# A two-layer attention kernel on one core: GpSimd's queue, x's transfers and the last batch's logits rearranged

## The chip, the core and the metric

The kernel runs on one core of one Trainium2 chip. The metric is device time in microseconds (us) of one execution; the time before is the median of three runs. One further execution was recorded by the hardware profiler, and all lines and durations below come from it.

## What is computed

The input x holds 8 batches of 32 x 32 positions (1024 tokens) with 512 channels, in float32. Two layers follow each other:

```python
x = x + layer0(gn(x))   # 16 heads of 32: softmax(q k / sqrt(32)) v, then w_proj + bias
x = x + layer1(gn(x))   # 4 heads of 128: softmax(q k / sqrt(128) + pos) v, then Wo
```

`gn` is a normalisation over groups of 16 channels and all positions: minus the mean, divided by the root of the variance. `pos` is a relative position logit: for a query at (x, y) and a key at (x', y') it is the sum of a term that depends on the query and x' and one that depends on the query and y'.

## The kernel before, in words

**Tiling and stages.** Activations lie transposed, channels on the 128 partitions, as blocks of 128 x 4 x 1024 (eight block buffers in SBUF). A projection of 512 x 512 is done by a scheme of seven products in place of eight (`seven`, L457), whose operands are sums of quarters of the activations (`forming`, L388, four VectorE sums, L414) and of quarters of the weights (made once, kept in DRAM, and streamed in for every use by `Stream`). Each product is 8 matmuls, 1.7 us of TensorE.

The first layer's attention (`attention_0`) takes 64 steps per batch: logits on TensorE (L762), exp on ScalarE (L777), the values' matmul (L788), and VectorE adds the exponentials (L800). The second layer's attention (`attention_1`) takes 64 blocks per batch (4 heads x 2 column halves x 8 key tiles): ScalarE copies the block's position logits into PSUM (L928), TensorE adds q k onto them (L969), ScalarE takes exp (L971), TensorE multiplies with the values (L982), VectorE adds the exponentials (L996, L998).

**Position logits** of a block are the sum of two broadcasts. `Seeds` first stores both terms of each head into DRAM, spread out (L884, two stores of 512 KB a head, names pc and pr). Then it loads per block one tile of 256 KB (row, pos<-pr, L915) and per eight blocks one of 256 KB (columns<-pc), and GpSimd adds them in place (L920). Row tiles lie in eight slots, which are the `pos` tile itself; therefore all four heads' stores must have read `pos` before its slots can be overwritten. `put(i)` copies row i to PSUM, loads row i + 8, and has the adds up to row i + 2 issued.

**What sets the order.** The loop over b runs 9 times. In turn b, attention_0 of batch b is the frame, and between its steps `side_by_side` deals out, by a planned total of work, the rest: projection and residual of batch b-1 (`after_0`), the output projection of batch b-2 (`after_1`), normalisation (`norm_1`), the second layer's projections (`second`), attention_1 of batch b-1, and the projections of batch b+1 (`before_0`). The 64 blocks of attention_1 count nothing, so they run as one stretch, 64 x 1.72 us. In that stretch `load` of batch b+1 is woven in: x by DMA (L288, 32 transfers of 64 KB a batch), transposed on VectorE (L1068), statistics (L301, L302), stored (L270), the normalisation (`group_norm`), and the four sums. In turn 7 there is no next batch, and half of attention_1 runs beside attention_0; turn 8 has only the second layer of batch 7, and `after_last` ends the kernel.

Each engine, and SyncE, which issues nearly all DMAs, works through its own queue in order. A scheduler at build time chooses that order from the order in the program, and `tc.issue_after(ins)` places an instruction behind another of the same engine. `stream.behind` is such an anchor for the weights' loads: before, every DMA of `Seeds` set it.

**Lines that the change touches.** `statistics` takes a fresh tile mv of two buffers per normalisation and clears it on GpSimd (L298); that memset must wait until VectorE has read the buffer's last contents (L327). `group_norm` takes the root on GpSimd (rstd, L342), and L346 applies it on VectorE. `normalise` ends with a multiply (L743) on GpSimd for the first layer and on VectorE for the second. `Onto.add` (L643, L645) adds a product's result to the residual on VectorE, and `put_out` transposes it (L1282) and stores it (L1287). In `after_last` the final projection starts with two products whose operands need no sums and goes on with five that do; `ends` holds the closing part of the last attention (sum over keys, L1015, reciprocal, L743).

Of the kernel before, what the change touches and what calls it, by code (L numbers as in the profile page):

```python
# [17 lines left out]
P = 128  # L18
# [9 lines left out]
def quick_path(  # L28
# [103 lines left out]


# [132 lines left out]
    def put_away(xT, name):  # L266
        kept = []
        for cc in range(CC):
            d = dram.tile([P, N], F32, tag="kept", name=f"d_{name}_{cc}", bufs=4 * CC)
            put[0] = nc.sync.dma_start(d, xT[cc])  # L270
            kept.append(d)
        return kept
# [21 lines left out]
    def statistics(st, xT, cc, name):  # L294

        if "mv" not in st:
            st["mv"] = small.tile([P, 32], F32, tag="mv", name=f"mv_{name}", bufs=2)
            nc.gpsimd.memset(st["mv"], 0.0)  # L298
        s = small.tile([P, NH, 6], F32, tag="st", name=f"st_{name}_{cc}", bufs=2)
        for h in range(NH):  # L300
            nc.vector.bn_stats(s[:, h, :], xT[cc][:, h * NB : (h + 1) * NB])  # L301
        nc.vector.bn_aggr(  # L302
            st["mv"][:, : 2 * CC].rearrange("p (s c) -> p c s", c=CC)[:, cc, :],
            s.rearrange("p h s -> p (h s)"),
        )

    def group_norm(st, xT, name, after=None, behind=None, out=None):
# [32 lines left out]
        )  # L340
        rstd = small.tile([P, CC], F32, tag="rstd", name=f"rstd_{name}")
        nc.gpsimd.tensor_tensor(rstd, var, neg_half, op=ALU.pow)  # L342
# [15 lines left out]
    in_place = [False]  # L358

# [202 lines left out]
    def in_two_parts(  # L562
# [7 lines left out]
        def products():  # L570
            if in_turn:

                base = stream.at + 1
                parts = [two_first(early, u, sinks[u], f"{name}_{u}") for u in range(2)]
                for i in range(4):
                    stream.at = base + i % 2
                    yield next(parts[i % 2])
                for part in parts:
                    try:
                        next(part)  # L580
                    except StopIteration as end:
                        p1s.append(end.value)
                return
            for u in range(2):
                stream.unit(m, False, u)
                p1s.append((yield from two_first(early, u, sinks[u], f"{name}_{u}")))
# [43 lines left out]
    class Onto:  # L630
# [9 lines left out]
        def add(self, n, h, t):  # L640
            part = self.dst[n][h]
            if self.bias is None:
                nc.vector.tensor_add(part, t, part)  # L643
            else:
                nc.vector.scalar_tensor_tensor(  # L645
                    part, t, self.bias[n], part, op0=ALU.add, op1=ALU.add
                )
# [220 lines left out]
    class Seeds:  # L868
# [4 lines left out]
        def __init__(self, pos, b):  # L873
            self.pos, self.b = pos, b
            self.kept = []
            self.rows, self.columns, self.summed = {}, {}, 0
            self.last = None
            for h in range(H1):

                by_columns = dram.tile([4, 32, N], F32, tag="pos", name=f"pc_{b}_{h}", bufs=4 * H1)  # L880
                by_rows = dram.tile([32, 4, N], F32, tag="pos", name=f"pr_{b}_{h}", bufs=4 * H1)
                for u, to in enumerate((by_columns.rearrange("i x n -> x i n"), by_rows)):
                    rows = pos[32 * u : 32 * u + 32, h, :]
                    nc.sync.dma_start(to, rows.unsqueeze(1).to_broadcast([32, 4, N]))  # L884
                self.kept.append(
                    (by_columns.rearrange("i x n -> (i x) n"), by_rows.rearrange("y i n -> (y i) n"))
                )
# [6 lines left out]

        def load(self, i):
# [3 lines left out]
            h, c = divmod(group, NH)  # L899
            by_columns, by_rows = [d[:, c * NB : (c + 1) * NB] for d in self.kept[h]]  # L900
# [6 lines left out]
            to = self.rows[i] = self.pos[:, at // NH, (at % NH) * NB : (at % NH + 1) * NB]  # L907
# [4 lines left out]
        def bring(self, to, rows):  # L912

            with tc.issue_after(self.last.ins) if self.last is not None else nullcontext():
                self.last = stream.behind = nc.sync.dma_start(to, rows)  # L915

        def add_up(self, upto):
            while self.summed < min(upto + 1, H1 * NH * NT):
                i = self.summed
                nc.gpsimd.tensor_tensor(  # L920
# [4 lines left out]
        def put(self, i, ps):  # L925
# [4 lines left out]
            self.add_up(i + 2)  # L930

    def attention_1(q, k, v, seeds, b, beside=0, ends=None):
# [71 lines left out]
        def finish(h, c, esum):  # L1004
# [10 lines left out]
            nc.tensor.matmul(su, fold_flat, few, start=True, stop=True)  # L1015
# [5 lines left out]
        for i, at in enumerate(steps):  # L1021
# [15 lines left out]
            if i > 5:  # L1037
                stream.release()
            yield 0
# [5 lines left out]
        else:  # L1045
            for _ in range(2):
# [5 lines left out]
    def load(b, st):  # L1052
# [4 lines left out]
        with tc.issue_after(put[0].ins) if b == 1 else nullcontext():  # L1057
# [16 lines left out]
        if b > 1:  # L1074
            st["xn"] = yield from forming(x, f"xn0_{b}", behind=lambda: added[0])
            return
# [5 lines left out]
        for _ in range(2):  # L1082
            yield next(sums)
# [132 lines left out]
    def second(b, st):  # L1216
# [35 lines left out]
        def spread():  # L1252
            seeds.append(Seeds(pos, b))
# [3 lines left out]
            keys_and_values, chain(turn_over(1), position_logits(q, turned, pos, b), spread()), 0, 1  # L1257
        )
        seeds[0].add_up(3)
# [103 lines left out]
    SECOND = 3 * PRODUCT - 8 - 1  # L1363
# [44 lines left out]
    for b in range(B + 1):  # L1408
# [8 lines left out]
        def forms_0_apart(b=b, st=here):  # L1417
            st["ao0"] = yield from forming(st["q0"], f"ao0_{b}")
# [4 lines left out]
        if last is not None:  # L1423
# [23 lines left out]
            total += SECOND  # L1447
            shared = here is not None and coming is None
# [19 lines left out]
            rest.append(woven(attention, incoming, 4, 5))  # L1468
# [22 lines left out]
    pf = bank("pf", [P, 1])[:D0]  # L1491
# [485 lines left out]
```

## Time and profile before

| | us |
|---|---|
| median of 3 runs | 3710.1 (3709.67 to 3711.36) |
| the profiled execution | 3716.11 |
| its span, first to last instruction | 3714.2 |
| mean granted TensorE clock | 0.995 of full speed |

| engine | busy us | what it does most |
|---|---|---|
| ScalarE (ACT) | 2030.6 | exp L777 961.9, exp L971 305.1, copy L928 296.8 |
| GpSimd (POOL) | 1291.6 | adds L920 732.8 (512 of 1460 ns) |
| DMA queue of SyncE (q1) | 40.4% of 16 engines | 398.33 MB |

The page of a profile gives busy time and share of the span for each engine, the span in 40 slices, the DMA queues, the chain of work that ended last, and groups of instructions with what ended the idle time before them. PE is TensorE's matmuls, PEld its weight loads, DVE is VectorE, SPq SyncE's queue. A line "A <- B: t, n, m" of the view of waits says that A sat idle t us in all, n times, at most m, until B was done. A timeline line gives start, duration, engine, source line, operation, out<-in, how many, and in brackets the idle time before it and what ended it. L375 is the matmul of every projection; its tile names (x_q, y_wo, z_v) tell the product group and the matrix.

### The profile page before, as it was taken

The page shows a single profiled execution, that of the slowest core. Times are in us where ns is not written, and L with a number is a line of the kernel's source. Part 1 is how long each engine was busy: PE and PEld are TensorE (multiplying, and loading weights), DVE is VectorE, ACT ScalarE, POOL GpSimd, SP SyncE. Part 2 cuts the span into 40 slices and gives each one's busy share as a digit, 9 for nine tenths or more (in the row PEclk, how much of TensorE's full clock was granted, in tenths as well). Part 3 has the DMA queues.
Part 4 walks back from the last instruction along what each step waited for, and adds up shares of the span by engine and source line. Part 5 has one row for each costly group of instructions (what it writes and reads, how often), then busy time and mean ns, then how long its engine had stood idle before and what let it go on. Part 6 is the DMA issues. An engine that isn't in the chain of part 4 may idle for free.

```text
span 3714.2 us, 81237 instructions
## 1 busy us (share of the span) xinstructions
PE 3654.9 (98%) x33998; PEld 1247.2 (34%) x33998; DVE 2565.8 (69%) x2905; ACT 2030.6 (55%) x2281; POOL 1291.6 (35%) x847
## 2 busy tenths in 40 slices
PE   9999999999999999999999999999999999999998
PEld 4232243222433234332343323423234232333343
DVE  6778667686676857769576685767858677666445
ACT  2555665446654466544665456654566445655343
POOL 1352155131551316413172132811337022255254
PEclk9999999999999999999999999999999999999999
DMA  6122174132842338334372343813457132334384
GB/s 191 62 87 90 41 179 138 60 109 63 192 131 93 84 78 204 95 95 97 99 195 70 101 91 97 217 51 100 92 126 199 39 115 60 104 111 135 103 218 105
DMA packets 575158, 419.40 MB, mean 113 GB/s; under 512 B 279840, under 2 KB 471616, under 8 KB 573760
## 3 DMA queue, kind: packets, MB, share of 16 engines
q1 hardware_dynamic: 563152, 398.33, 40.4%
q0 software_dynamic: 2608, 13.70, 1.0%
q8 instruction: 270, 4.42, 0.5%
q10 hardware_dynamic: 9024, 2.10, 0.3%
q14 instruction: 104, 0.85, 0.1%
HBM read 321.72 MB, written 92.27 MB: 111 GB/s over the span
## 4 chain that ended last, share of the span: by engine, by line
PE 89%; DVE 5%; ACT 2%; DMA 2%; issue 1%; POOL 1%; SPq 1%; ACTq 0%; DVEq 0%; POOLq 0%
PE ps L762 14%; PE acc L788 13%; PE ps L969 10%; PE acc L982 10%; PE y_q L375 4%; PE y_k L375 4%; PE y_v L375 4%; PE z_q L375 3%; PE x_k L375 3%; PE x_q L375 3%; PE x_v L375 3%; PE z_k L375 3%; PE z_v L375 3%; PE y_wp L375 2%; PE y_wo L375 2%; PE x_wp L375 2%
## 5 line engine op out<-in xcount | busy, mean ns | idle before, releaser
L800 DVE TENSOR_TENSOR e_room<-e_room 128x2048 f32<-128x2048 f32 x448 | 1083.1, 2418 | 445.6 <-ACT e_room L777 443.1
L777 ACT ACTIVATE e_room<-ps 128x2048 f32<-128x2048 f32 x512 | 961.9, 1879 | 747.6 <-PE ps L762 716.7
L920 POOL TENSOR_TENSOR pos<-pos,columns 128x512 f32<-128x512 f32 x512 | 732.8, 1460 | 197.4 <-DMA pos<-pr 196.6
L762 PE MATMUL ps<-q,k 32*64 32x512 f32 x8192 | 594.6, 613 | 2.3 <-ACT e_room L777 2.3
L788 PE MATMUL acc<-e_room,v 128*32 128x512 f32 x4096 | 546.8, 604 | 1.0 <-ACT e_room L777 1.0
L982 PE MATMUL acc<-e,v 128*128 128x512 f32 x1024 | 527.1, 598 | 15.0 <-ACT e L971 14.5
L969 PE MATMUL ps<-q,k 128*128 128x512 f32 x1024 | 533.5, 604 | 6.7 <-ACT ps L928 6.6
L971 ACT ACTIVATE e<-ps 128x512 f32<-128x512 f32 x512 | 305.1, 597 | 267.6 <-PE ps L969 248.9
L998 DVE TENSOR_TENSOR es<-es,e 128x512 f32<-128x512 f32 x384 | 274.7, 715 | 159.8 <-ACT e L971 154.8
L928 ACT COPY ps<-pos 128x512 f32<-128x512 f32 x512 | 296.8, 590 | 75.0 <-POOL pos L920 36.2
L743 POOL TENSOR_TENSOR q<-q,su 128x512 f32<-128x512 f32 x64 | 104.6, 1634 | 528.8 <-DVE su L739 525.5
L982 PEld LDWEIGHTS acc<-e,v 128*128 128x128 f32 x1024 | 193.1, 191 | 269.9 <-issue 207.2
L969 PEld LDWEIGHTS ps<-q,k 128*128 128x128 f32 x1024 | 187.8, 191 | 242.5 <-issue 207.6
L762 PEld LDWEIGHTS ps<-q,k 32*64 32x64 f32 x8192 | 123.3, 129 | 398.2 <-issue 220.9
L788 PEld LDWEIGHTS acc<-e_room,v 128*32 128x32 f32 x4096 | 81.4, 108 | 412.2 <-issue 363.0
L628 POOL TENSOR_TENSOR k<-b_k,p_k 128x512 f32<-128x512 f32 x32 | 48.9, 1527 | 481.6 <-ACT p_k L479 481.6
L628 POOL TENSOR_TENSOR q<-b_q,p_q 128x512 f32<-128x512 f32 x32 | 60.2, 1881 | 384.3 <-ACT p_q L479 360.4
L628 POOL TENSOR_TENSOR v<-b_v,p_v 128x512 f32<-128x512 f32 x32 | 56.8, 1775 | 349.3 <-ACT p_v L479 349.3
L860 ACT COPY pos<-pp 32x512 f32<-32x512 f32 x128 | 104.3, 815 | 29.5 <-PE pp L851 28.3
L996 DVE TENSOR_TENSOR es<-e,e 128x512 f32<-128x512 f32 x64 | 74.3, 1161 | 63.7 <-ACT e L971 63.7
L704 DVE STREAM_TRANSPOSE tu<-su 128x512 f32<-128x512 f32 x64 | 45.1, 705 | 90.1 <-ACT su L702 90.1
L375 PE MATMUL y_q<-f_xn,w_q 128*32 128x512 f32 x768 | 92.9, 602 | 2.4 <-DVE a_q L465 2.4
(225 smaller groups left out, 4457.8 us busy)
## 6 DMA issues: line engine op xcount, KB each, us to landing
pos<-pr SPq DMA_DIRECT2D x512, 256.0 KB, 4.5
w_qkv<-ws_qkv SPq DMA_DIRECT2D x168, 128.0 KB, 2.6
d<-x0T SPq DMA_DIRECT2D x32, 512.0 KB, 5.1
x1T<-d SPq DMA_DIRECT2D x32, 512.0 KB, 5.1
d<-x1T SPq DMA_DIRECT2D x32, 512.0 KB, 3.5
pc<-pos SPq DMA_DIRECT2D x32, 512.0 KB, 7.0
pr<-pos SPq DMA_DIRECT2D x32, 512.0 KB, 8.2
columns<-pc SPq DMA_DIRECT2D x64, 256.0 KB, 5.3
```

What stands on the lines that cost most here:

```text
L375: ins = nc.tensor.matmul(out[columns, :], weights[:, columns], moving, start=start, stop=stop, skip_group_check=open_sum,)
L628: nc.gpsimd.tensor_tensor(self.dst[1][1], s(b), s(p7), op=ALU.add)
L762: nc.tensor.matmul(ps[some, r, :], k[m][rows, j * P + 64 * i : j * P + 64 * i + 64], q[m][rows, h * NB : (h + 1) * NB], start=True, stop=True,
L777: exps[0] = nc.scalar.activation(e, ps, AF.Exp, scale=D0 ** -0.5)
L788: nc.tensor.matmul(acc[r * D0 : (r + 1) * D0, :], v[:, j, c0 : c0 + D0], e[:, r, :], start=(j == blocks[0]), stop=(j == blocks[-1]),)
L800: summed[0] = nc.vector.tensor_add(state["esum"], state["esum"], e)
L920: nc.gpsimd.tensor_tensor(self.rows[i], self.rows[i], self.columns[i // NT], op=ALU.add)
L928: nc.scalar.copy(ps, rows)
L969: scored[0] = nc.tensor.matmul(ps, k[h][:, keys], q[:, h, queries], start=False, stop=True, skip_group_check=True)
L971: nc.scalar.activation(e, ps, AF.Exp, scale=1.0 / math.sqrt(D1))
L982: nc.tensor.matmul(acc, v[:, j, h * D1 : (h + 1) * D1], e, start=(j == 0), stop=(j == NT - 1),)
L998: added[0] = nc.vector.tensor_add(state["esum"], state["esum"], e)
```

## The change

- The mv tiles become two constant tiles, cleared once at the start and used in turn; the 16 memsets at L298 go.
- For batches 2 to 7 `load` is replaced by `load_apart`: three portions of x (4 transfers each) are fetched first and one after each transposed portion, each behind `stream.behind`; each quarter is stored as soon as it is transposed; the root on GpSimd is issued behind the newest logits add; the fourth sum moves to the start of `before_0`. The weaving into attention_1 goes from every fifth block to two of every seven.
- `put(i)` has the logits' adds issued up to row i + 4, not i + 2, and six before the attention, not four.
- `Seeds` takes an own block as room for the rows of the last batch; there only head 0 is stored before the first eight rows are loaded, and head h + 1 at the third row of head h. `stream.behind` is now set once per attention block, to the newest `Seeds` DMA.
- In the end: the closing part of attention_1 goes one step further before it is handed on (three steps, not two), its sums' matmul and the first products keep their order, the residual adds of the second pair of products stand behind the newest sum, and the verdict's matmul gets a PSUM room of its own.
- The sums between the two layers of batch 7 stand behind the newest softmax add, and the planned work grows by one unit where there is no previous or no next batch.

```diff
@@ consts
+    mvs = [consts.tile([P, 32], F32, tag=f"mv{i}", name=f"mv{i}") for i in range(2)]
+    for t in mvs:
+        nc.gpsimd.memset(t, 0.0)
@@ statistics
-            st["mv"] = small.tile([P, 32], F32, tag="mv", name=f"mv_{name}", bufs=2)
-            nc.gpsimd.memset(st["mv"], 0.0)
+            st["mv"] = mvs[0]
+            mvs.reverse()
@@ group_norm(..., apart=False)
+        if apart:
+            yield 0
         rstd = small.tile([P, CC], F32, tag="rstd", name=f"rstd_{name}")
-        nc.gpsimd.tensor_tensor(rstd, var, neg_half, op=ALU.pow)
+        with tc.issue_after(spread[0].ins) if apart else nullcontext():
+            nc.gpsimd.tensor_tensor(rstd, var, neg_half, op=ALU.pow)
@@ in_two_parts, in_turn
                 for i in range(4):
                     stream.at = base + i % 2
+                    if i == 0:
+                        in_place[0] = True
+                    behind_sums[0] = i > 1
                     yield next(parts[i % 2])
+                behind_sums[0] = False
@@ Onto.add
-                nc.vector.tensor_add(part, t, part)
+                with tc.issue_after(last_form[0].ins) if behind_sums[0] else nullcontext():
+                    nc.vector.tensor_add(part, t, part)
@@ Seeds
+            self.room = pos if room is None else room
...
+            if room is not None:
+                self.put_by(0)
+                for i in range(self.ROWS):
+                    self.load(i)
+                return
...
+            if h == len(self.kept) - 1 and h + 1 < H1 and c == 0 and j == 2:
+                self.put_by(h + 1)
...
-                self.last = stream.behind = nc.sync.dma_start(to, rows)
+                self.last = nc.sync.dma_start(to, rows)
...
-            self.add_up(i + 2)
+            self.add_up(i + 4)
@@ attention_1
-            nc.tensor.matmul(su, fold_flat, few, start=True, stop=True)
+            ins = nc.tensor.matmul(su, fold_flat, few, start=True, stop=True)
+            if ends is not None and (h, c) == steps[-1][:2]:
+                tc.keep_in_program_order(ins)
+                in_place[0] = True
...
+            stream.behind = seeds.last
...
-            for _ in range(2):
+            for _ in range(3):
                 next(last)
@@
+    def load_apart(b, st, parts):
+        def bring(i):
+            with tc.issue_after(stream.behind.ins):
+                return load_blocks(b, *parts[i])
+        ahead = [bring(i) for i in range(3)]
+        yield 0
+        x = block(f"x0T_{b}")
+        xT = chunks(x)
+        st["kept"] = []
+        for i, (cc, h) in enumerate(parts):
+            nc.vector.transpose(xT[cc][:, h * NB : (h + 1) * NB], ahead.pop(0))
+            if h == NH - 1:
+                statistics(st, xT, cc, f"0_{b}")
+                st["kept"] += put_away(xT[cc : cc + 1], f"0_{b}_{cc}")
+            yield 0
+            if i + 3 < len(parts):
+                ahead.append(bring(i + 3))
+        late = lambda: added[0]
+        yield from group_norm(st, xT, f"0_{b}", apart=True)
+        fs = st["xn"] = []
+        sums = st["sums0"] = forming(x, f"xn0_{b}", behind=late, into=fs)
+        for _ in range(3):
+            yield next(sums)
@@ second
-            seeds.append(Seeds(pos, b))
+            seeds.append(Seeds(pos, b, block(f"slots_{b}") if b == B - 1 else None))
...
-        seeds[0].add_up(3)
+        seeds[0].add_up(5)
@@ the loop over b
-            st["ao0"] = yield from forming(st["q0"], f"ao0_{b}")
+            st["ao0"] = yield from forming(st["q0"], f"ao0_{b}", behind=lambda: added[0])
...
-            rest.append(woven(attention, incoming, 4, 5))
+            if here is not None and coming is not None:
+                rest.append(woven(attention, incoming, 3, 7, (0, 4)))
+            else:
+                rest.append(woven(attention, incoming, 4, 5))
```

## The prediction

> **What bounds the kernel now.** I read the page first (busy shares), then TensorE's waits, then the timeline around each of those waits, and last the granted clock there. The page's first part:
>
> ```profile
> PE 3654.9 (98%) x33998; PEld 1247.2 (34%) x33998; DVE 2565.8 (69%) x2905; ACT 2030.6 (55%) x2281; POOL 1291.6 (35%) x847
> ```
>
> TensorE is busy 3654.9 of 3714.2 us. No edit removes a matmul, so only its idle time and slow time can be won. The view of waits, for TensorE (what it waited for: total, times, longest):
>
> ```profile
> PE acc L982 <- ACT e L971: 14.5, 8, 3.1
> PE ps L969 <- ACT ps L928: 6.6, 14, 1.3
> ...
> PE z_v L375 <- DMA w_v<-ws_v: 3.0, 1, 3.0
> PE sums L1015 <- DVE fw L712: 2.7, 1, 2.7
> ...
> PE y_wo L375 <- DVE f_wo L414: 2.2, 1, 2.2
> ```
>
> The top row is the second layer's attention: acc waits for exp. Within 960 to 3080 us it is five waits of about 1.84 us, one per batch, and at 572 us one of 3.07. The GpSimd timeline just ahead of the one at 1480 us shows who is late:
>
> ```profile
> 1463.31 3.89 POOL L920 TENSOR_TENSOR pos<-pos,columns 128x512 f32<-128x512 f32 x3
> 1473.69 0.12 POOL L298 MEMSET mv<- 128x32 f32 x1 [6.50 <-DVE turned L327]
> 1473.77 3.73 POOL L920 TENSOR_TENSOR pos<-pos,columns 128x512 f32<-128x512 f32 x3
> 1479.07 1.02 POOL L342 TENSOR_TENSOR rstd<-var,neg_half 128x4 f32<-128x4 f32 x1 [1.57 <-DVE var L338]
> ```
>
> A 0.12 us memset holds GpSimd for 6.50 us, the root for 1.57 + 1.02, and the logits' adds (L920) stand behind both. ScalarE's copy of the summed logits (L928) then waits 2.71 us at 1481.36, and its exp stands behind that copy. The last view is TensorE by stretches (length, TensorE busy, ..., granted clock, DMA share, GB/s):
>
> ```profile
> 569.00:582.00 13.00, 9.89 (x16) 3.77 (x15) 9.19 (x14) 6.35 (x12) 11.42 (x9) 0.74 0.92 285
> ...
> 1479.00:1485.00 6.00, 4.15 (x11) 1.65 (x10) 3.95 (x5) 3.31 (x6) 5.93 (x5) 1.00 0.92 306
> ...
> 3360.00:3374.00 14.00, 9.87 (x18) 4.11 (x17) 13.09 (x16) 4.34 (x8) 13.16 (x8) 0.76 0.48 136
> 3541.00:3564.00 23.00, 16.08 (x126) 6.51 (x119) 4.49 (x6) 6.56 (x12) 15.37 (x13) 0.85 0.74 207
> ...
> 3680.00:3704.00 24.00, 20.09 (x174) 5.59 (x166) 15.30 (x22) 1.17 (x2) 6.00 (x4) 0.93 0.39 56
> ```
>
> A wait of 1.85 us leaves the clock at 1.00, longer ones (3.07 at 572, 2.66 at 3365, 3.00 at 3549, 2.24 at 3681) are followed by half speed. A mean of 0.74 over 13 us is 2 x 0.26 x 13 = 6.8 us at half clock, so 3.4 us lost beside the wait; 3360 to 3374 likewise 3.4, 3541 to 3564 3.4, 3680 to 3704 1.7.
>
> The Trainium skill, "TensorE: Matmul & The Clock Gate", section "HAM oscillation", has the rule that idle gaps over about 3.4 us throttle TensorE. By it none of these gaps would, and my sum below would be smaller by the clock terms I count, 3.4 + about 2.6 + 1.7. The rows differ from it, and I go by the rows.
>
> **The change, part by part** (times of the profiled execution: span 3714.2, run 3716.1).
>
> *Memset and root (six batches).* The memsets waited 8.61, 4.53, 6.50, 4.02, 5.56 and 4.79 us in the six phases that prepare a later batch; two tiles cleared once leave no wait. The root now stands behind the last add traced. Behind the root's result stand only the normalising instructions (L346), traced three to four blocks of 1.72 us later, so its delay is hidden; if it were not, VectorE's sums, exp and TensorE would queue behind L346. Won: 3.07 + 3.4 at 572 us, and 5 x 1.84. **15.7.** Next late would be the row transfers: GpSimd waits for them 196.6 us in 129 waits, but the 4.20 us one at 1456.67 cost TensorE nothing. Bounds 12 to 16.
>
> *Adds four blocks ahead.* Here GpSimd's queue holds hardly anything but these adds, so a greater lead changes little; adds 4 and 5 now precede the 3.32 us multiply (L743) at 1419.36. Against it: in the stage of batch 7's first layer, L743 then stands behind adds that wait up to 4.9 us for rows. **0**, bounds 2 won to 3 lost.
>
> *x in portions.* Before, 20 of the 32 x transfers of a batch were issued from 1425 to 1458 and 12 earlier, beside the projections; now all 32 stand behind row transfers, 12 at once in block 3, then 4 every three to four blocks, and three of the four stores of x0T move forward. From 1420 to 1475 SyncE issued 63 transfers at about 0.55 us, 35 of 55 us; 15 more make 43. It fits. The transfer engines are tighter: share 0.91 at 204 GB/s; 12 x 64 KB + 3 x 512 KB = 2.3 MB are 11 us at that rate, 7.7 us at the 306 GB/s of 1479 to 1485. So rows come up to 6 us later (50 + 11 against 55). The cover: adds done by 1467.19 were copied at 1471.29 to 1473.52, and copies run ahead of their matmuls. Without cover a batch pays a wait like 1.84 or 3.07 + 3.4. Bounds 0 to 6 x 6.5; I take **2 lost** in total, nearest the row in which a 4.20 us delay was hidden. VectorE gets lighter there by one sum (L414, 1.2 to 1.8 us each), which moves beside the next projection's first product.
>
> *The last batch's own slots.* SyncE's timeline before:
>
> ```profile
> 3526.70 2.85 SPq L884 DMA_DIRECT2D pr<-pos  x1
> 3529.65 2.49 SPq L915 DMA_DIRECT2D columns<-pc  x1
> 3532.23 3.62 SPq L915 DMA_DIRECT2D pos<-pr  x2
> ...
> 3544.34 1.06 SPq L226 DMA_DIRECT2D w_v<-ws_v  x2
> ```
>
> Six stores go before the first row, eight before the value weights, which are ordered behind the rows (stream.behind) and land too late for z_v. TensorE loses 3.2 (ps) + 3.0 (w_v) + 0.7 (acc) + 3.4 (clock) = 10.3. Now the first row needs the first head's two stores only (issued 3519.09 and 3520.28), and the order behind rows is gone for these weights. Bytes ahead of the eighth row fall from 8 x 512 + 9 x 256 KB = 6.4 to 4.4 MB, at 195 GB/s 10 us less: it lands near 3541, when the attention starts. I take **8**; bounds 10.3 won to 3 lost: heads 2 and 3 are stored in blocks 10 and 26, 1 MB each, 5 us at the 209 GB/s of 3565 to 3640. Four waits of ps for copies there (2.4 us) may go by the earlier adds: **1**, bounds 0 to 2.4.
>
> *Tail.* VectorE before the last projection's second part:
>
> ```profile
> 3678.88 1.00 DVE L743 TENSOR_TENSOR q<-q,su 128x512 f32<-128x512 f32 x1
> ...
> 3679.87 0.68 DVE L643 TENSOR_TENSOR x2T<-x_wo,x2T 128x512 f32<-128x512 f32 x1
> 3680.47 1.21 DVE L414 TENSOR_TENSOR f_wo<-q 128x1024 f32<-128x1024 f32 x1
> 3681.60 0.70 DVE L1282 STREAM_TRANSPOSE ot<-x2T 128x512 f32<-128x512 f32 x1
> 3682.23 1.18 DVE L414 TENSOR_TENSOR f_wo<-f_wo,q 128x1024 f32<-128x1024 f32 x1
> ```
>
> y_wo waits for the second sum, done 3683.41, while TensorE is free at 3681.22. The sums' matmul comes one product (1.7 us) earlier, and the add and transpose (0.68 + 0.70) go behind the sums: ready about 3680.5. That ends 2.24 + 1.7; I take **3.5**, bounds 0 to 3.9. The 1.67 us wait of z_wo for ScalarE, which is issuing stores, stays.
>
> *Batch 7's first layer.* At 3358.70 the first sum (L414) holds VectorE 2.38 us for GpSimd's L743; TensorE then loses 1.5 + 2.7 + 3.4. The sum now stands behind the newest softmax add, so less is queued behind it, but it can still wait. I take **2**, bounds 3 lost to 7.6 won. One unit more of planned work in two stages and the verdict's own PSUM room: 0, within 1 either way.
>
> Sum: 15.7 + 0 - 2 + 8 + 1 + 3.5 + 2 = 28.2; 3716.1 - 28.2 = 3687.9. The profiled run is 6.0 above the median of 3710.1, so on the medians 3681.9: **3682**.
>
> **Rivals.**
> 1. *Transfers become the bound, mildly*: rows late by some 2.3 us of TensorE time per batch, clock kept: 6 x 2.3 = 14 more, 3696. For it: DMA share 0.91 and the 11 us above. Against: the hidden 4.20 us.
> 2. *The other side, slower*: the same place (blocks 8 to 30 of six attention phases), waits long enough to halve the clock. Price 3.3 + 3.4 = 6.7 per batch, 40 in all; without my 2, 3682 - 2 + 40 = 3720. It decides from (28 + 2) / 6 = 5.0 us lost per batch. Against it: rows are eight blocks ahead, 13.8 us, against 4.6 us to land.
> 3. *It does not do what it says*: the five short waits stay, because exp still stands behind a copy that waits for a late row, and the own slots bring nothing: 3682 + 9.2 + 8 = 3699.
> 4. *Little change*: memsets gone (15.7), but the end turns worse: the spread stores cost 3, batch 7's sums 3, the x loads 4, the tail gains nothing: 3710.1 - 15.7 + 10 = 3704.
>
> **How the numbers follow.** Chances: forecast 0.63, rival 1 0.14, rival 3 0.09, rival 4 0.07, rival 2 0.07. The low end is all bounds won, 16 + 2 + 10.3 + 2.4 + 3.9 + 7.6 = 42: 3668. The high end takes in rival 4: 3705; rival 2 is left out. A measurement tells 0.2% (7.4 us) from no change: under 3702.7 is faster (forecast, 1, 3: 0.86), rival 4 is the same (0.07), rival 2 slower (0.07).
>
> **What would show it.** Right: no wait of GpSimd for turned (L327) and none of acc near block 36 of each batch; clock 1.00 at 569 to 582; w_v issued before 3537 and no z_v wait; y_wo without its 2.2 us. Wrong: acc or ps waits around blocks 10 to 30, GpSimd's waits for pos<-pr well over 196.6 us, a half clock in each batch; or the last batch's ps waiting later on.

## The result, and the profile after

| | median of the runs | profiled execution |
|---|---|---|
| before | 3709.9 us (3703.2 to 3713.9, 12 runs) | 3716.1, span 3714.2 |
| after | 3720.2 us (3715.9 to 3722.1, 12 runs) | 3721.6, span 3719.7 |

The ratio is 1.0026, 95% interval 1.0017 to 1.0035: the change makes the kernel slower, by a little over 0.2%, where I had forecast 3682. Both times lie outside each other's range, and the forecast's range ended at 3705. The traced execution of the kernel before is slower than each of its 12 timed ones (its mean granted clock is 0.995, that of the trace after 0.997), so the two traces differ by 5.5 us only, the medians by 10.3.

Starts of the same exp in the two traces, subtracted, tell where it goes. The changed kernel is 0.5 us late before batch 1's second attention, loses 5.3 to 7.2 us more from each attention to the next, and stands 32.6 us late where batch 7's turn begins (3006.3 us before, 3039.0 after). Then it wins: 17.8 late at the last block of batch 6's attention, 8.4 at the last block of batch 7's, 5.5 at the end. So a gain of 27 us is there. It is eaten by what was lost ahead of it.

The page after, first part. TensorE's busy time is what it was; its time without work is 66.0 us (3719.7 - 3653.7), 59.3 before:

```profile
PE 3653.7 (98%) x33998; PEld 1243.8 (33%) x33998; DVE 2558.4 (69%) x2905; ACT 2025.6 (54%) x2281; POOL 1282.1 (34%) x833
```

Each kernel has its own line numbers. In the changed one the root is L350 (L342 before), the normalising L354 (L346), the key sum L727 (L712), the logits' add L946 (L920), ScalarE's copy L954 (L928), exp L997 (L971) and the softmax add L1024 (L998). TensorE's waits after (what for: total, times, longest):

```profile
PE ps L995 <- ACT ps L954: 16.5, 38, 1.2
PE sums L1041 <- DVE fw L727: 15.3, 12, 1.5
PE acc L1008 <- ACT e L997: 8.1, 13, 1.1
...
PE y_q L385 <- DVE a_q L475: 0.6, 1, 0.6
...
PE y_wo L385 <- DVE f_wo L424: 0.5, 1, 0.5
```

The old long waits are gone or short (acc was 14.5 with a longest of 3.1, y_q 2.4, y_wo 2.2, z_v is missing). Many shorter waits are there instead: ps for ScalarE's copies 38 times (0.4 us on average), sums for the key sums 12 times (1.3 us on average).

GpSimd in the same batch as before, around the root (start, length, ..., idle before and its releaser):

```profile
1487.64 7.12 POOL L946 TENSOR_TENSOR pos<-pos,columns 128x512 f32<-128x512 f32 x5 [0.20 <-DMA pos<-pr]
1496.92 3.83 POOL L946 TENSOR_TENSOR pos<-pos,columns 128x512 f32<-128x512 f32 x3 [2.16 <-DMA pos<-pr]
1500.71 1.02 POOL L350 TENSOR_TENSOR rstd<-var,neg_half 128x4 f32<-128x4 f32 x1
```

No memset waits, and the root waits for nothing of its own. But its input, the variance, was ready at 1496.5, and three adds stood ahead of it, which had just waited 2.16 us for a row. VectorE meanwhile:

```profile
1496.36 0.16 DVE L343 SCALAR_TENSOR_TENSOR var<-back 128x4 f32<-128x4 f32 x1
1496.44 2.30 DVE L1024 TENSOR_TENSOR es<-es,e 128x512 f32<-128x512 f32 x3
1501.77 1.75 DVE L354 TENSOR_SCALAR x0T<-x0T,back,rstd 128x1024 f32<-128x1024 f32 x1 [3.03 <-POOL rstd L350]
1503.44 0.69 DVE L1024 TENSOR_TENSOR es<-es,e 128x512 f32<-128x512 f32 x1
...
1507.42 1.12 DVE L354 TENSOR_SCALAR x0T<-x0T,back,rstd 128x1024 f32<-128x1024 f32 x1
1508.46 0.67 DVE L727 TENSOR_REDUCE fw<-tu 128x16 f32<-128x512 f32 x1
```

The first normalising instruction (L354) holds VectorE for 3.03 us, and softmax adds (L1024) and the key sum (L727) stand in its queue behind it. TensorE then waits 0.73 (acc), 1.48 (sums) and 0.42 us (acc) between 1504 and 1511. Its longest wait there, and VectorE's view of waits for this pair, which had 0.3 us before:

```profile
1509.19 0.40 PE L1041 MATMUL sums<-fw,fold 128*128 128x16 f32 x2 [1.48 <-DVE fw L727]
...
DVE x0T L354 <- POOL rstd L350: 17.2, 7, 3.4
```

The granted clock, in stretches that answer to those of before, and one more (the clock is the third number from the end):

```profile
569.00:582.00 13.00, 12.81 (x32) 5.78 (x32) 10.06 (x25) 9.54 (x18) 10.35 (x9) 1.00 0.78 213
...
1964.00:1972.00 8.00, 6.92 (x14) 3.05 (x15) 6.26 (x12) 3.79 (x7) 8.00 (x6) 0.79 0.41 130
3410.00:3424.00 14.00, 14.00 (x36) 6.35 (x35) 11.79 (x17) 9.94 (x17) 9.77 (x8) 1.00 0.58 183
3563.00:3586.00 23.00, 22.63 (x86) 10.12 (x79) 12.41 (x17) 15.73 (x27) 21.05 (x17) 1.00 0.67 185
```

The drops at 572, in batch 7's turn and at the last attention's start are gone. A new one, 3.4 us long (8 x 0.21 x 2) and 1.7 us lost, follows the cluster of waits in batches 3, 4 and 5, at 1966, 2423 and 2880, and none in batches 0 to 2.

SyncE at the last attention's start:

```profile
3541.40 0.96 SPq L231 DMA_DIRECT2D w_v<-ws_v  x1
3543.75 1.16 SPq L941 DMA_DIRECT2D slots<-pr  x2
3544.97 0.58 SPq L941 DMA_DIRECT2D pc<-pos  x1
3545.59 0.56 SPq L941 DMA_DIRECT2D pr<-pos  x1
3546.20 7.16 SPq L941 DMA_DIRECT2D slots<-pr  x6
```

The value weights are no longer behind eight stores: the second head's stores (L941, pc and pr) come later than they do, and TensorE no longer waits for them. And VectorE in the tail (the last projection), where the sums now go ahead of the add and transpose:

```profile
3685.58 1.05 DVE L758 TENSOR_TENSOR q<-q,su 128x512 f32<-128x512 f32 x1
...
3686.67 1.23 DVE L424 TENSOR_TENSOR f_wo<-q 128x1024 f32<-128x1024 f32 x1
3687.93 2.18 DVE L424 TENSOR_TENSOR f_wo<-f_wo,q 128x1024 f32<-128x1024 f32 x1
3690.04 0.68 DVE L658 TENSOR_TENSOR x2T<-x_wo,x2T 128x512 f32<-128x512 f32 x1
```

The sums now follow the multiply (L758) closely, and y_wo waits 0.5 us instead of 2.2, although the second sum takes 2.18 us where it took 1.18.

### The profile page after: what moved, and what is told of

It reads as the page before. It is cut to its first block, busy times and chain, and to the rows that moved or that the text cites. A ratio compares the mean times of both kernels' runs of the same rounds, so it can differ in the third digit from the quotient of the medians.

```text
span 3719.7 us, 81204 instructions
## 1 busy us (share of the span) xinstructions
PE 3653.7 (98%) x33998; PEld 1243.8 (33%) x33998; DVE 2558.4 (69%) x2905; ACT 2025.6 (54%) x2281; POOL 1282.1 (34%) x833
## 4 chain that ended last, share of the span: by engine, by line
PE 90%; DVE 3%; ACT 2%; POOL 2%; issue 2%; DMA 1%; SPq 0%; ACTq 0%; DVEq 0%; POOLq 0%
PE ps L777 14%; PE acc L803 13%; PE ps L995 10%; PE acc L1008 9%; PE y_v L385 4%; PE y_q L385 4%; PE y_k L385 4%; PE x_v L385 3%; PE z_q L385 3%; PE x_k L385 3%; PE x_q L385 3%; PE z_k L385 3%; PE z_v L385 3%; PE y_wp L385 2%; PE y_wo L385 2%; PE sums L825 2%
## 5 line engine op out<-in xcount | busy, mean ns | idle before, releaser
L946 POOL TENSOR_TENSOR pos<-pos,columns 128x512 f32<-128x512 f32 x448 | 640.5, 1454 | 212.4 <-DMA pos<-pr 205.6
L995 PE MATMUL ps<-q,k 128*128 128x512 f32 x1024 | 534.6, 605 | 16.5 <-ACT ps L954 16.5
L997 ACT ACTIVATE e<-ps 128x512 f32<-128x512 f32 x512 | 305.4, 597 | 310.2 <-PE ps L995 268.8
L1024 DVE TENSOR_TENSOR es<-es,e 128x512 f32<-128x512 f32 x384 | 278.0, 724 | 188.2 <-ACT e L997 181.2
L758 POOL TENSOR_TENSOR q<-q,su 128x512 f32<-128x512 f32 x64 | 107.2, 1674 | 558.0 <-DVE su L754 533.3
L954 ACT COPY ps<-pos 128x512 f32<-128x512 f32 x448 | 256.0, 590 | 36.9 <-PE ps L967 9.2
L719 DVE STREAM_TRANSPOSE tu<-su 128x512 f32<-128x512 f32 x64 | 45.2, 706 | 87.4 <-ACT su L717 87.2
L385 PE MATMUL y_q<-f_xn,w_q 128*32 128x512 f32 x768 | 91.3, 593 | 0.8 <-DVE a_q L475 0.6
```

The lines of the kernel that those rows point to most:

```text
L385: ins = nc.tensor.matmul(out[columns, :], weights[:, columns], moving, start=start, stop=stop, skip_group_check=open_sum,)
L946: spread[0] = nc.gpsimd.tensor_tensor(self.rows[i], self.rows[i], self.columns[i // NT], op=ALU.add)
L954: nc.scalar.copy(ps, rows)
L995: scored[0] = nc.tensor.matmul(ps, k[h][:, keys], q[:, h, queries], start=False, stop=True, skip_group_check=True)
L997: nc.scalar.activation(e, ps, AF.Exp, scale=1.0 / math.sqrt(D1))
L1024: added[0] = nc.vector.tensor_add(state["esum"], state["esum"], e)
```

## The experiments

My theory after the traces: the new preparation of x (portions, their order behind rows, root and sums placed anew) costs the 33 us; slots, tail and batch 7's turn win theirs. The rival: the adds four ahead, or full transfers, make logits late. A difference of some 3 us between two kernels lies within the runs' spread, so for those the traces are read as well.

**1. Preparation as before.**

```diff
-        if b > 1:
-            yield from load_apart(b, st, parts)
-            return
...
+        if b > 1:
+            st["xn"] = yield from forming(x, f"xn0_{b}", behind=lambda: added[0])
+            return
...
-                rest.append(woven(attention, incoming, 3, 7, (0, 4)))
+                rest.append(woven(attention, incoming, 4, 5))
```

> The changed kernel with the whole preparation of a later batch's x put back as it was before: the x transfers unordered, two portions ahead, the four stores together, root and normalising instructions free, the fourth sum in the attention; constant mv tiles, adds four ahead, the last batch's own slots and the tail stay. My theory: the loss of 32.7 us that the trace of the change shows from batch 1 to batch 6 comes from this preparation alone, and the 27 us won in batch 7's turn and at the end from the other parts, so 3720 - 33 = 3687 us (3680 to 3695). Rival (the adds four ahead, or GpSimd's queue as a whole, cost the time): little comes back, 3705 to 3720.

3671.8 us, ratio to before 0.9895 (0.9879 to 0.9911): 48.4 under the changed kernel. The preparation is the cause, and costs more than the 33 us that I read from the comparison with before, since that comparison already held gains: where batch 7's turn begins, this run is 16.6 us ahead of the kernel before (memsets and planned work, runs 6 and 14). This version beats both kernels. GpSimd's waits for rows fall to 161.9 us (205.6 after, 196.6 before).

**2. Portions of x not ordered behind rows.**

```diff
-            with tc.issue_after(stream.behind.ins):
+            with nullcontext():
                 return load_blocks(b, *parts[i])
```

> The changed kernel, but the portions of x are not ordered behind the row transfers. My theory: this order makes the scheduler place ScalarE's copies of the logits late and in bunches, right ahead of the exp that needs them, and TensorE waits for ps about 1.9 to 2.4 us a batch; without it the waits of ps for copies go and 6 x 1.9 to 2.4 = 12 to 14 us come back: 3707 us (3702 to 3712). The waits of acc and sums around the root stay. Rival (the rows themselves land late because the transfers and SyncE are full): no gain, or worse, 3718 to 3730, since x now goes ahead of rows.

3702.3 us, 0.9983 (0.9974 to 0.9992): 17.9 come back. TensorE's waits of ps for copies fall from 16.5 us in 38, while GpSimd waits for rows as long as in the changed kernel (205.6 us):

```profile
PE ps L995 <- ACT ps L954: 4.2, 14, 1.2
...
POOL pos L946 <- DMA pos<-pr: 204.6, 129, 6.7
```

So it was not late rows that cost this time. ScalarE in the changed kernel (blocks 22 to 24), and at blocks 22 and 23 in this one:

```profile
1466.66 0.60 ACT L997 ACTIVATE e<-ps 128x512 f32<-128x512 f32 x1 [0.63 <-PE ps L995]
1468.38 0.60 ACT L997 ACTIVATE e<-ps 128x512 f32<-128x512 f32 x1 [1.12 <-PE ps L995]
1470.10 0.60 ACT L997 ACTIVATE e<-ps 128x512 f32<-128x512 f32 x1 [1.12 <-PE ps L995]
1470.95 0.59 ACT L1027 COPY q<-acc 128x512 f32<-128x512 f32 x1 [0.26 <-PE acc L1008]
1471.44 1.63 ACT L954 COPY ps<-pos 128x512 f32<-128x512 f32 x3
```

```profile
1461.10 0.59 ACT L954 COPY ps<-pos 128x512 f32<-128x512 f32 x1
1462.13 0.60 ACT L997 ACTIVATE e<-ps 128x512 f32<-128x512 f32 x1 [0.44 <-PE ps L995]
1462.81 0.59 ACT L954 COPY ps<-pos 128x512 f32<-128x512 f32 x1
1463.85 0.60 ACT L997 ACTIVATE e<-ps 128x512 f32<-128x512 f32 x1 [0.44 <-PE ps L995]
```

Without the order one copy goes between two exps. With it ScalarE idles 1.12 us, twice, between exps that have no copy between them, and then does three copies in a row behind the copy of acc (L1027), with nothing that they wait for; their adds had been done 2.9 to 4.3 us earlier. So it is their place in ScalarE's queue that is late. Counted over the traces, the order is the same in all six attentions: in the changed kernel only one copy is left ahead at exps 13, 20, 24, 27, 31 and 34, in this run at 31 and 34, in the kernel before in most at exp 24 alone. That is what an order fixed when the program is built looks like. By the same exps, 3.0 us return by block 36 of each attention; behind it 1.3 to 3.1 us are lost again in batches 0, 1 and 2, where VectorE now waits up to 4.8 us for the root (25.8 us in 7 waits).

**3. Normalising behind the softmax add of its block.**

```diff
-        yield from group_norm(st, xT, f"0_{b}", apart=True)
+        yield from group_norm(st, xT, f"0_{b}", behind=late, apart=True)
```

> The changed kernel, but the four normalising instructions are ordered behind the softmax add of their own block. My theory: in the change the first of them stands right behind the variance on VectorE and holds it about 3 us while GpSimd's root waits behind adds that wait for rows; the softmax adds and key sums queue behind it, TensorE waits 2.6 us a batch for them and runs at half clock for 3.4 us in three of six batches (1.7 us lost each). So 6 x 2.6 + 3 x 1.7 = 21 us come back: 3699 us (3695 to 3708). Rival (VectorE's hold is hidden and the waits come from late copies): 3715 to 3722.

3700.7 us, 0.9978 (0.9969 to 0.9988): 19.4 come back, 2.0 to 4.9 us in the second half of each attention. The root's place is as it was; five softmax adds stand ahead of L354 now, and its wait at the same place is 1.06 us:

```profile
1492.28 3.90 DVE L1024 TENSOR_TENSOR es<-es,e 128x512 f32<-128x512 f32 x5
1497.24 1.75 DVE L354 TENSOR_SCALAR x0T<-x0T,back,rstd 128x1024 f32<-128x1024 f32 x1 [1.06 <-POOL rstd L350]
```

**4. All four sums in the attention.**

```diff
-        for _ in range(3):
+        for _ in range(4):
             yield next(sums)
```

> The changed kernel, but all four sums of the next batch's first factors are put into the attention, as before, and none beside the next projection. My theory: the placement at the end of the attention, ahead of the last key sums on VectorE, costs a wait of 1.07 us a batch: 6 x 1.07 = 6 us come back, 3714 us (3711 to 3718), if the fourth sum then finds a gap. Rival (the placement costs nothing): 3718 to 3722.

3717.1 us, 1.0019 (1.0010 to 1.0029): 3.1 come back, half of what I expected, inside its range and within the runs' spread. The waits of sums fall from 15.3 to 8.9 us and those of acc rise from 8.1 to 12.0. This alone decides nothing; run 13 does.

**5. The edits of 2 and 3 together.**

> The changed kernel with both of the edits of the second and third run: x not ordered behind the rows, and the normalising instructions ordered behind the softmax add of their block; x in portions of two, the spread stores and the sums stay. My theory: the two costs are separate. Copies placed late cost 3.0 us in the first half of each attention (traces of the second run), VectorE held behind the root 2.2 to 4.6 us in the second half, and what the second run gave back in the second half (1.4 to 3.1 in three batches) was that hold alone, so both together give at least the sum: 3720 - 18 - 19 = 3683 us, down to 3676 without the part given back. Rival (one cause seen twice): 3695 to 3700, no better than either alone.

3681.5 us, 0.9925 (0.9913 to 0.9938). They add up (17.9 + 19.4 = 37.3; 38.6 measured): two separate costs.

**6. Before, with constant mv tiles alone.**

```diff
-            st["mv"] = small.tile([P, 32], F32, tag="mv", name=f"mv_{name}", bufs=2)
-            nc.gpsimd.memset(st["mv"], 0.0)
+            st["mv"] = mvs[0]
+            mvs.reverse()
```

> The kernel before with one edit alone: two constant mv tiles in place of a memset per use. My prediction's first term: 15.7 us won (12 to 16), so 3709 - 15.7 = 3693 us; the first run of this study, which also had the adds four ahead, was 15.9 us ahead of the kernel before where batch 7's turn begins. Rival (the root, or the lead of the adds, is what holds the logits, and the memset alone is worth little): 3704 to 3709.

3697.2 us, 0.9967 (0.9955 to 0.9979): 11.7 won. The trace has the 5.2 us at 572 and gains of about 1.8 us in three later batches, but 1.7 us are lost in two of them, in one place to a new wait of acc of 1.46 us. GpSimd now meets at the root what it met at the memset, 25.5 us before:

```profile
POOL rstd L346 <- DVE var L342: 48.0, 16, 5.9
```

Of acc's five waits from 960 to 3080 us (9.2 us) four are left, 4.7 us.

**7. Adds two ahead, on the kernel of run 1.**

```diff
-            self.add_up(i + 4)
+            self.add_up(i + 2)
...
-        seeds[0].add_up(5)
+        seeds[0].add_up(3)
```

> The kernel of the first run (3671.8 us) with the logits added two blocks ahead, as before. My prediction's term: nothing (2 lost to 3 won), so 3672 us (3669 to 3674). Rival (the lead is what ends the late copies in batch 7's turn, where 14.9 us were won against a forecast of 2): 3680 to 3687.

3670.2 us, 0.9897 (0.9882 to 0.9911), 1.6 under run 1 and within its spread; the traces differ by 0.8 us at the end of batch 7's attention. The lead is worth nothing that can be measured, and the rival falls. This is the fastest version measured.

**8. Batch 7's first-layer sums free again, on the kernel of run 1.**

```diff
-            st["ao0"] = yield from forming(st["q0"], f"ao0_{b}", behind=lambda: added[0])
+            st["ao0"] = yield from forming(st["q0"], f"ao0_{b}")
```

> The kernel of the first run (3671.8 us) with batch 7's first-layer sums no longer ordered behind the newest softmax add. My theory: the sum that held VectorE at 3358 us in the kernel before is set free by this order, so most of the 14.9 us won in that turn go again: 3680 to 3687 us. Rival (the adds four ahead won them): 3670 to 3674.

3674.4 us, 0.9908 (0.9893 to 0.9922): 2.6 lost, within the spread, of which the trace shows 1.4 at the place. My theory that this order won batch 7's 14.9 us falls.

**9. No own slots, on the kernel of run 1.**

```diff
-            seeds.append(Seeds(pos, b, block(f"slots_{b}") if b == B - 1 else None))
+            seeds.append(Seeds(pos, b))
...
-                self.last = nc.sync.dma_start(to, rows)
+                self.last = stream.behind = nc.sync.dma_start(to, rows)
```

> The kernel of the first run (3671.8 us) without the last batch's own slots: all stores of the logits ahead of the first row, rows into the logits' own tile, and weights ordered behind the newest row, as before. My prediction's term is 8 us (10.3 to -3), and the trace of the first run wins 14.8 us between blocks 0 and 16 of the last attention, of which 4.4 were lost just ahead: 3680 to 3683 us. Rival (the own slots are not what frees the start): 3671 to 3674.

3679.7 us, 0.9920 (0.9907 to 0.9934): 7.9 lost. By the exps 11.8 go between blocks 0 and 16 of the last attention and 4.4 come back just ahead. The 4.4 are work that moved: 96 matmuls of the value projection (L385) run ahead of the first exp in run 1 and behind it here. Of the 7.4 us that are left, 5.4 are waits: ps 1.25 and 1.19, z_v for its weights 1.09, acc 2.24, against 0.38 (acc) in run 1.

**10. The tail's old order, on the kernel of run 1.**

```diff
-            if ends is not None and (h, c) == steps[-1][:2]:
-                tc.keep_in_program_order(ins)
-                in_place[0] = True
...
-            for _ in range(3):
+            for _ in range(2):
                 next(last)
...
-                    if i == 0:
-                        in_place[0] = True
-                    behind_sums[0] = i > 1
```

> The kernel of the first run (3671.8 us) with the tail's order as before: the last key sum free, two steps of it in the attention, the last projection's adds free. My prediction's term: 3.5 us (0 to 3.9), so 3675 us (3673 to 3677). Rival (the tail's order moves only what was hidden): 3670 to 3673.

3671.1 us, 0.9898 (0.9883 to 0.9913): nothing lost that can be measured. TensorE's wait for f_wo is back at 2.2 us, but no half clock follows it. The next wait, of z_wo for ScalarE's p_wo, is 0.93 us; with the new order it is two, 0.35 and between 0.62 and 1.54 us. From the last exp to the end it is 39.8 us here and 40.2 in run 1, but 38.5 to 39.8 in the 12 other traces with the new order: it may win about 1 us. The four traces with the old order and a half clock behind this wait have 41.3 to 42.2.

**11. One unit less of planned work, on the kernel of run 1.**

```diff
-    SECOND = 3 * PRODUCT - 8
+    SECOND = 3 * PRODUCT - 8 - 1
...
-            if past is not None and coming is not None:
-                total -= 1
```

> The kernel of the first run (3671.8 us) with the planned work of one product stage one unit less, as before (which changes only the pace at which the two streams of batch 7's turn and of batch 1's turn are woven). I predicted nothing for it. Neither the order behind the softmax add (2.6 us) nor the adds four ahead (none) accounts for the 14.9 us won in batch 7's turn, so my theory now: the pace does, 3680 to 3686 us. Rival (the freed order of the weights behind the rows, tried in another run beside this one, wins them): 3670 to 3674.

3679.0 us, 0.9920 (0.9906 to 0.9933): 7.2 lost, in batch 1's turn and in batch 7's. This number only sets how fast the products of one stream advance beside the other's blocks. The y_q wait of 2.08 us in batch 7's turn is back.

**12. The root free, in the changed kernel.**

```diff
-        with tc.issue_after(spread[0].ins) if apart else nullcontext():
+        with nullcontext():
             nc.gpsimd.tensor_tensor(rstd, var, neg_half, op=ALU.pow)
```

> The changed kernel, but the root isn't ordered behind the newest add of logits. It then stands eight adds earlier in GpSimd's queue. If the order of the root is what holds VectorE (my theory), VectorE's 3 us wait ends and the time is that of the third run, 3700 us (3696 to 3706). Rival (the normalising instructions right behind the variance are what holds VectorE, wherever the root stands, since adds that wait for rows are ahead of it in any place): 3712 to 3722.

3753.4 us, 1.0119 (1.0103 to 1.0134): 33 slower still. Both theories fall. The root stands eight adds earlier and waits on GpSimd for the variance, the old fault enlarged:

```profile
1506.77 1.02 POOL L350 TENSOR_TENSOR rstd<-var,neg_half 128x4 f32<-128x4 f32 x1 [8.13 <-DVE var L343]
1507.76 12.85 POOL L946 TENSOR_TENSOR pos<-pos,columns 128x512 f32<-128x512 f32 x9
```

The adds behind it come late, ScalarE's copies and exps after them, and TensorE waits for exp:

```profile
PE acc L1008 <- ACT e L997: 46.4, 7, 7.7
```

So in this preparation the root has to be ordered. What is wrong in the change is the instruction on VectorE that waits for it.

**13. Run 5 with all four sums in the attention.**

> The kernel of the fifth run (3681.5 us) with all four sums of the next batch's factors in the attention. My theory: the fourth sum ahead of the last key sums costs a wait of 1.0 us a batch, as the trace of the change shows, hidden in the fourth run by the hold behind the root: 3681.5 - 6 = 3675.5 us (3673 to 3678). Rival (the sum's place costs nothing or the fourth sum in the attention costs as much): 3680 to 3684.

3674.5 us, 0.9906 (0.9893 to 0.9920): 7.0 under run 5, by the exps 1.0 us in each of six batches. The fourth sum's place is the third cost. In the changed kernel it stands on VectorE ahead of the last key sum:

```profile
1545.57 1.22 DVE L424 TENSOR_TENSOR f_xn<-x0T,f_xn 128x1024 f32<-128x1024 f32 x1
1546.70 0.71 DVE L726 STREAM_TRANSPOSE tu<-es 128x512 f32<-128x512 f32 x1
1547.45 0.69 DVE L727 TENSOR_REDUCE fw<-tu 128x16 f32<-128x512 f32 x1
```

and TensorE waits 1.07 us for that key sum at 1547.

**14. Before, with the unit of planned work alone** (the edit of 11, reversed).

> The kernel before with one edit alone: the planned work of the product stage one unit more, in the two turns where the change has it so. By removal from the first run the pace is worth 7.2 us, in batch 1's turn and batch 7's turn. My theory: it is worth as much here, 3710 - 7 = 3703 us (3700 to 3705). Rival (it pays only once the memsets are gone): 3706 to 3712.

3694.4 us, 0.9963 (0.9950 to 0.9977): 16.0 won, over twice what removal had shown. It is the largest gain of any one part, from one unit in a count. By the exps 6.9 us are won by the end of batch 1's turn, where the wait at 572 is 1.85 us instead of 3.07 and no half clock follows, and 13.5 in batch 7's. There y_q's 2.08 us wait with its half clock is 0.63, acc's 1.48 is gone, and the 2.66 of sums, with its half clock, is this:

```profile
PE sums L1015 <- DVE fw L712: 1.0, 1, 1.0
```

**15. Before, with mv tiles and the unit.**

> The kernel before with the constant mv tiles and the pace together. If they add up: 3710 - 11.7 - 7.2 = 3691 us. My theory is that each removes waits that set off a half clock in the other's turn, so together they win some 5 us more, 3684 to 3688 us. Rival (they simply add, and the 10 us lie elsewhere): 3690 to 3693.

3684.9 us, 0.9936 (0.9922 to 0.9949): 25.5 won. The number is the one I expected and the reason is not: 11.7 + 16.0 = 27.7, so they do not help each other; both clear the half clock at 572.

**16. Root and normalising both placed apart, on the kernel of run 7.**

```diff
-        yield from group_norm(st, xT, f"0_{b}")
+        yield from group_norm(
+            st, xT, f"0_{b}", behind=(lambda: added[0]) if b > 1 else None, apart=b > 1
+        )
```

> The kernel of the seventh run (3670.2 us: x prepared as before, two adds ahead) with the root one step after the variance and behind the newest add of logits, and the normalising instructions behind the newest softmax add. My theory: the wait of GpSimd for the variance (4.8 us in the first run's trace, 45 us in 16 waits) goes without a wait of VectorE for the root, and the waits of acc for exp near block 40 go with it: 3666 to 3669 us. Rival (those waits are hidden, or come back as VectorE's): 3669 to 3676.

3676.0 us, 0.9911 (0.9898 to 0.9925): 5.8 slower than run 7, so my theory falls. GpSimd's waits for the variance fall from 45.2 to 28.1 us, and VectorE's for the root stay at 0.3, but neither had cost much in run 7, where TensorE waits 0.8 us for acc in all. The last sum of the factors now starts at 1523.4, right ahead of the last key sum, where run 7 had it at 1514.7, and the third cost is back: TensorE's view has a row that run 7 has not,

```profile
PE sums L1041 <- DVE fw L727: 6.4, 6, 1.1
```

1.0 us in each of six batches. Whether the added step or one of the two orders moved that sum was not tried.

## Why the prediction was wrong

| term | forecast, us won | measured | runs |
|---|---|---|---|
| memsets | 15.7, with the root | 11.7 | 6 against before |
| root behind the adds | hidden (no own term) | -19.4 with L354 where it stands | 3 |
| adds four ahead | 0 | -1.6, in the spread | 7 |
| x behind the rows | -2 | -17.9 | 2 |
| fourth sum beside the projection | 0 | -7.0 | 13 against 5 |
| own slots | 8 | 7.9 | 9 |
| copies in the last attention | 1 | 0: ps waits 2.4 us in both traces | before, after |
| tail | 3.5 | -0.7, in the spread | 10 |
| batch 7's sums | 2 | 2.6, in the spread, the trace 1.4 | 8 |
| one unit of planned work | 0, within 1 | 16.0 alone, 7.2 by removal | 14, 11 |

The measured terms close: before 3710 - 25.5 (memsets and unit, run 15) - 7.9 - 2.6 = 3674, run 1 is 3671.8; with 17.9 + 19.4 + 7.0 on top, 3716, and the changed kernel is 3720.2. The 4 us that are missing (2.7 of them between runs 13 and 1) are not assigned.

**The step that failed** is "Behind the root's result stand only the normalising instructions (L346), traced three to four blocks of 1.72 us later, so its delay is hidden". I took the distance between variance and normalising from the trace of before and held it fixed:

```profile
1478.77 0.16 DVE L338 SCALAR_TENSOR_TENSOR var<-back 128x4 f32<-128x4 f32 x1
...
1484.24 1.76 DVE L346 TENSOR_SCALAR x0T<-x0T,back,rstd 128x1024 f32<-128x1024 f32 x1
```

Here 5.3 us lie between the two. The change rebuilt that stretch: the normalising instruction stands only three softmax adds behind the variance and is reached 2.2 us after it, and the root stands behind three logits' adds, the first of which waits for a row. The same sentence goes on to name just what then happened ("VectorE's sums, exp and TensorE would queue behind L346"), with no price. Run 3 shows the cost, 19.4 us, and run 12 that in this preparation a root without the order costs more still.

**The second**: "rows come up to 6 us later", with copies that "run ahead of their matmuls" as the cover. The cover was the loss. GpSimd does wait longer for rows than with the old preparation (205.6 us, run 1 161.9), but that is hidden: with 204.6 in run 2 the waits of ps went all the same, and run 13, with 198.5, is only 2.7 us slower than run 1. What cost 17.9 us was the copies' place in ScalarE's queue, and the sign that the prediction gave for being wrong, waits of ps around blocks 10 to 30, is there. Why the build places them so when x is ordered behind rows was not tried.

**The third**: I counted the fourth sum, which "moves beside the next projection's first product", only as work taken off VectorE. I did not look at what would stand behind it in VectorE's queue: the last key sum, for which TensorE waits.

**Right by mechanism**: the memsets' waits are gone, though for less than the bounds of 12 to 16, as a free root takes over part of them (run 6); the slots (8, measured 7.9, in the waits that I had named); the lead of the adds. The order of batch 7's sums is too small to tell. **Wrong to the good**: the unit of planned work, waved through at "0, within 1 either way". It decides which blocks of the two streams meet in a turn, and the waits of y_q, acc and sums in batch 7's turn and the one at 572 hang on that. I had put the last, with its half clock, down to the memset alone; either edit clears the half clock and part of the wait (3.07 to 1.1 in run 6, 1.85 in run 14). The tail's wait went as described, from 2.2 to 0.5 us; of that a new wait of z_wo took 0.35, and the half clock that I had counted in does not follow the wait in run 10.

Rival 2 named 3720, the measured time, in the right stage. That is luck: its cause, late rows, was hidden, and in the trace half clocks follow in three batches, not in six. Taken at its word it would have led to the wrong repair (smaller transfers), while unordered transfers, one argument on the normalising, and `range(4)` bring 46 us.

## What to carry to other kernels

- An edit that reorders a queue moves everything queued behind it. The distance that hides a wait must be taken from the new order; where it can't be, price the wait as if bare and keep that end in the range.
- When two engines exchange a small result, a wait taken off one queue can come up on the other. Both ends, the producer's place and the consumer's, have to be moved past the work that the bound engine needs.
- A count that only sets the pace of two woven streams can be worth more than the edits beside it. Such a unit is cheap to try alone.

## What the runs showed of the hardware

The clock does not follow from the length of one wait, as I had read it (1.85 us harmless, 2.24 us and more followed by half speed). In the changed kernel the waits at 1504 to 1511 us (0.73, 1.48, 0.42) leave the clock at 1.00; nearly the same ones a batch later, at 1960 to 1966 (0.80, 1.47, 0.42), are followed by 3.4 us at half clock. The first lines are the changed kernel's, the last that of run 12, behind its wait of 7.67 us:

```profile
1499.00:1507.00 8.00, 7.27 (x17) 2.94 (x17) 5.23 (x6) 5.09 (x9) 8.00 (x7) 1.00 1.01 261
1507.00:1516.00 9.00, 7.10 (x18) 2.91 (x17) 8.38 (x14) 4.85 (x9) 9.00 (x7) 1.00 0.48 154
...
1964.00:1968.00 4.00, 2.92 (x6) 1.36 (x7) 3.76 (x9) 2.05 (x4) 4.00 (x4) 0.77 0.20 64
1968.00:1972.00 4.00, 4.00 (x9) 1.70 (x8) 2.50 (x4) 1.75 (x4) 4.00 (x4) 0.81 0.62 197
```

```profile
1512.00:1520.00 8.00, 8.00 (x16) 3.49 (x17) 5.56 (x7) 5.09 (x9) 8.00 (x7) 0.81 0.60 171
```

The same wait goes both ways, too. The y_q wait of 2.08 us is followed by 3.4 us at half clock in the trace of before and by none in runs 6 and 11; the f_wo wait of 2.24 us by 3.4 us in before and in runs 6, 14 and 15 and by none, at 2.23 us, in run 10. And one program differs between its executions: beside run 1 the kernel before took from 3703.8 us at a mean clock of 0.998 to 3715.9 us at 0.995. Lost clock of 0.003 over 3710 us is 11 us, by this estimate nearly all of the difference. So a clock term read from one execution, as in my sum, is not a fixed price of a wait.

The Trainium skill, "TensorE: Matmul & The Clock Gate", section "HAM oscillation", gives idle gaps over about 3.4 us as what throttles; run 12's gap is over that and agrees, the cluster of batch 3, with no gap over 1.5 us, does not. What decides between the two clusters, or between two executions, is open.
